# A state-space block followed by an attention-convolution block: scan matmuls on the two halves of the array's rows, and another form of the LayerNorm pass

## The chip, the core and the metric

The kernel runs on one core of a Trainium2 chip. Five engines work side by side, each through its own queue in order: PE (matmuls; PEld is its weight load), DVE (VectorE), ACT (ScalarE), POOL (GpSimd) and SP (SyncE), which here issues nearly all DMAs. The metric is the device time of one execution in microseconds; three runs of the kernel before gave 7110.56 to 7121.52, with a median of 7116.44.

## The reference, cut to what matters

Four images of 96 channels and 128 x 128 pixels pass through two blocks.

```python
# block 1, per image: d = 192 inner channels, L = 128*128
z  = silu(depthwise3x3(in_w @ x))
xs = [z, z^T, flip(z), flip(z^T)]                 # 4 directions k
dts, B, C = split(x_proj[k] @ xs[k], (6, 1, 1))
delta = softplus(dt_w[k] @ dts + dt_b[k])         # 192 channels from 6 rows
h_t = exp(-exp(A_log)*delta_t) * h_(t-1) + delta_t * B_t * xs_t
y   = sum over k of (h * C + D * xs), each turned back
x1  = x + out_w @ layernorm_over_channels(y) + out_b
# block 2, per image: normalise x1, split it by sign (relu_split_norm),
# two 3x3 convolutions make keys and queries, their products make a 3x3
# kernel per image, which convolves a third map; output = several terms summed
```

## The kernel before

**Block 1, projections.** `project` makes z of one image in strips of 8 rows (128 x 512 fp32 matmuls, line 601), stores it (`zb`), and makes the 16 small rows per direction pair that the scans need (`rows_out`, `cols_out`). These are kept as three bf16 pieces whose sum is the fp32 value: `xdt` (6 rows of dt for each direction) and `xbc` (B and C), both in DRAM.

**Block 1, scans.** `ssm_scan` works on pairs of images. The 384 channels of a pair are three groups of 128: group 0 is of the first image alone, group 1 is half of each image, group 2 is of the second image alone. Each group has 4 directions with 16 chunks of 1024 positions: 64 steps a group, 384 steps in all for two pairs, 256 of them of one image alone and 128 of both. Two steps share one load of rows, `xr` (`rows_in`, 4 buffers, issued six steps ahead), and one load of z, `u` (`u_in`). Each step has two halves of 512 positions. Per half there are three matmuls: `pd` = dt (line 750, in `deltas`), and B and C spread over the 128 channels (line 776, in `spread`, PSUM tiles `pBC`, 3 buffers). The contraction holds 60 rows for one image (9 x 6 rows for the three-piece products and 6 for B and C) and 120 for two. So `xr` is loaded by three DMAs of 18 rows and one of 6 rows for each image, each row 2048 positions (4 KB): 4 DMAs for a pair of steps of one image, 8 for a pair of both. After the matmuls: softplus and exp on ACT, three DVE operations per half (lines 803, 820 the scan itself, 824), and two POOL operations per step (799 and 832).

**LayerNorm pass.** `ssm_output` handles one image in 16 chunks of 1024 positions. Of each chunk it forms means of y and y^2 over 192 channels (matmuls with `mean192`, line 927), copies them (937), regroups them by two small DMAs (940, `mq`), makes the reciprocal root (944 to 954), writes it to DRAM (956, `rd`), reads it back broadcast over 96 partitions (964, `r`), and scales the projected chunk (978 to 980). Three chunks are in work at once: the loop body starts chunk c, makes the root of chunk c-1 and projects and scales chunk c-2; y is loaded three chunks ahead. The result goes to `xr` and from there to `xnew` (1015).

**Split norm.** `split_norm` reads `xnew` twice in 16 pieces, the first time for sums (lines 1064 to 1071), the second time to write the two signed maps `x1d`, `x2d` (1139 to 1154). Pieces are loaded three ahead, in 4 buffers, the first ones before the small arithmetic that precedes each pass.

**Order of work.** Generators are interleaved by `co_run(left, right, pace)`: each `yield` of `left` states a cost, and `right` is advanced by that cost times `pace`. A scan step costs 5.2. The scans run beside the projections of images 0, 1 and 2-3 (pace 0.25, 0.75, 1.35), then beside `norm` of image 0, that is `ssm_output` and `split_norm` (pace 0.5), then beside `direct_maps` of image 0 (pace 0.95); what is left is drained. All these instructions keep the order in which they were emitted on each engine (`in_order`). After that come `attend` of images 0 to 3, each with the `norm` of the next image and the output stage of the last one beside it; there the framework's scheduler orders the instructions, with the order of emission as priority.

**Setup.** `scan_weights` fills `wdt` and `wbc` by DMAs that POOL issues (lines 233 and 236); `output_weights` and the first strip of `project` follow.

Of the kernel before, what the change touches and what calls it, by code (L numbers as in the profile page):

```python
# [17 lines left out]
C = 96  # L18
# [42 lines left out]
def kernel(  # L61
# [151 lines left out]
    def scan_weights():  # L213


        wdt = const.tile([KS, 3, NK, 128], BF16, name="wdt", tag="wdt")
        wbc = const.tile([KS, 3, 2, 128], BF16, name="wbc", tag="wbc")
        with tc.tile_pool(name="w0", bufs=1) as w0:
# [8 lines left out]
            for img, ch, g, p, n in PARTS:  # L227
                row = img * KI if g == 1 else 0
                for w in range(3):
                    src = pieces[w].rearrange("p (k c) -> p k c", k=NK)[:, :, ch : ch + n]  # L230
                    for i in range(3):
                        at = row + w * 18 + i * RANK
                        nc.gpsimd.dma_start(wdt[at : at + RANK, g, :, p : p + n], src)
                for q in range(2):
                    at = row + 54 + q
                    nc.gpsimd.dma_start(wbc[at : at + 5 : 2, g, q, p : p + n], one[:, :n])
# [170 lines left out]
    def project(b, weights, stats, beside, zb, xdt, xbc, ps):  # L407
# [9 lines left out]
        with tc.tile_pool(name="a2", bufs=2, side="left") as p2:  # L417
# [81 lines left out]
            def rows_out(z1, z2, s):  # L499
# [26 lines left out]
                def store():  # L526
                    for q in range(2):
                        sl = slice((2 * s + q) * CH, (2 * s + q + 1) * CH)
                        for dst, p, n in ((xdt, 0, 12), (xbc, 12, 4)):
                            at = 32 * q + p  # L530
                            nc.sync.dma_start(
                                dst[0, :, :, sl].rearrange("i r f -> r i f"), rp[at : at + n]
                            )
# [7 lines left out]
            def cols_out(rp, s):  # L541
# [16 lines left out]
                def store():  # L558
                    h = (s - HS + 1) * ZR
                    for dst, r, n in ((xdt, 0, 12), (xbc, 12, 4)):  # L560
                        for i in range(3):
                            to = dst[1, i].rearrange("r (w h) -> w r h", h=H)
# [82 lines left out]
    def ssm_scan(zb, xdt, xbc, yms, ready):  # L645
# [5 lines left out]
        with (  # L651
# [32 lines left out]
            def rows_in(n):  # L684

                if n >= total:
                    return
                g, k = steps[n][:2]
                sl = slice(lows(n) * SN, (lows(n) + 2) * SN)
                imgs = images(g)  # L690
                xr = p1.tile([KS, 2 * SN], BF16, name="xr", bufs=4)
                for a, img in enumerate(imgs):
                    at = a * KI
                    r = k // 2 * RANK
                    src = xdt[img][k % 2, :, r : r + RANK, sl]
                    for w in range(3):
                        nc.sync.dma_start(xr[at + 18 * w : at + 18 * w + 18], src)
                    r = k // 2 * 2
                    src = xbc[img][k % 2, :, r : r + 2, sl]
                    nc.sync.dma_start(xr[at + 54 : at + KI], src)  # L700
                pairs[n] = dict(xr=xr[0 : KI * len(imgs)])
# [35 lines left out]
            def deltas(n):  # L737
                if n >= total:
                    return
                g, k, i, c = steps[n][:4]  # L740
# [4 lines left out]
                xr = pairs[n - n % 2]["xr"]  # L745
                at = (c - lows(n - n % 2)) * SN
                for half in range(2):
                    pd = ps.tile([128, CH], F32, name="pd", bufs=2)
                    sl = slice(at + half * CH, at + half * CH + CH)
                    nc.tensor.matmul(  # L750
                        pd, lhsT=wdt[0 : xr.shape[0], g % 3, k], rhs=xr[:, sl],
                        start=True, stop=True,
                    )
# [17 lines left out]
            def spread(n, q, half):  # L771

                xr = pairs[n - n % 2]["xr"]
                p = ps.tile([128, CH], F32, name="pBC", bufs=3)
                at = (steps[n][3] - lows(n - n % 2)) * SN + half * CH
                nc.tensor.matmul(  # L776
                    p,
                    lhsT=wbc[0 : xr.shape[0], steps[n][0] % 3, q],
                    rhs=xr[:, at : at + CH],
                    start=True,  # L780
                    stop=True,
                )
# [118 lines left out]
    def ssm_output(b, yms, xnew, stats, ps, side):  # L901
# [4 lines left out]

        with tc.tile_pool(name="c2", bufs=2, side=side) as p2:
# [3 lines left out]
            ys, sums_of, near, made = {}, {}, {}, {}  # L911
# [6 lines left out]
            def squares(c):  # L918
                sq = p2.tile([C, 2, SN], F32, name="sq", bufs=1)
                for j in range(2):  # L920
                    nc.scalar.activation(sq[:, j], ys[c][:, j], AF.Square)
                sums_of[c] = sq, bank(ps)

            def sums(c, j):
                sq, pm = sums_of[c]
                for g in range(4):
                    nc.tensor.matmul(
                        pm[32 * g : 32 * g + 32],
                        lhsT=mean192[:, 0:32],
                        rhs=(ys[c], sq)[g % 2][:, j, bass.ts(g // 2, CH)],  # L930
                        start=(j == 0),
                        stop=(j == 1),
                    )

            def rows(c):
                st = p2.tile([128, CH], F32, name="st", bufs=1)
                nc.scalar.copy(st, sums_of.pop(c)[1])
                mq = made[c] = p2.tile([RS, 2, W], F32, name="mq")
                for i in range(2):
                    nc.sync.dma_start(mq[:, i], st[32 * i : 32 * i + 65 : 64])  # L940

            def inverse(c):
                m, q = made[c][:, 0], made[c][:, 1]
                nc.vector.tensor_mul(m, m, m)
                nc.vector.tensor_sub(q, q, m)
                nc.vector.tensor_scalar(q, q, 0.0, None, ALU.max)

            def roots(c):
                q = made[c][:, 1]
                nc.scalar.activation(q, q, AF.Sqrt, bias=eps[0:RS])  # L950

            def back(c):
                q = made.pop(c)[:, 1]
                nc.vector.reciprocal(q, q)
                to = rd[bass.ts(c, SN)]
                nc.sync.dma_start(to.rearrange("(p f) -> p f", f=W), q)
                xr = p2.tile([C, SN], F32, name="xr")
                nc.sync.dma_start(xr, xb[:, bass.ts(c, SN)])
                near[c] = xr, to

            def spread_out(c):
                xr, to = near[c]
                r = p2.tile([C, SN], F32, name="r")
                nc.sync.dma_start(r, to.partition_broadcast(C))
                near[c] = xr, r

            def projected(c, h):
                po = part(ps, C, CH)
                for j in range(2):
                    nc.tensor.matmul(  # L970
                        po, lhsT=outws[:, j], rhs=ys[c][:, j, bass.ts(h, CH)],
                        start=(j == 0), stop=(j == 1),
                    )
                return po

            def scaled(c, h, po):
                xr, r = (t[:, bass.ts(h, CH)] for t in near[c])
                nc.vector.tensor_mul(r, po, r)
                nc.vector.scalar_tensor_tensor(xr, r, outbs, xr, ALU.add, ALU.add)
                nc.vector.bn_stats(stats[:, 2 * c + h], xr)  # L980

            for c in range(3):
                load_y(c)
            yield 2.0
            for c in range(NS + 2):
                new, old = c < NS, c - 2 if c >= 2 else None
                mid = c - 1 if 1 <= c <= NS else None
                if old is not None:
                    po = projected(old, 0)
                yield 1.2  # L990
                if mid is not None:
                    inverse(mid)
                    roots(mid)
                if new:
                    squares(c)
                if old is not None:
                    scaled(old, 0, po)
                    po = projected(old, 1)
                    ys.pop(old)
                if mid is not None:  # L1000
                    back(mid)
                yield 1.4
                if new:
                    sums(c, 0)
                if mid is not None:
                    spread_out(mid)
                yield 1.4
                if old is not None:
                    scaled(old, 1, po)
                    load_y(c + 1)  # L1010
                if new:
                    sums(c, 1)
                yield 1.4
                if old is not None:
                    nc.sync.dma_start(xnew[:, bass.ts(old, SN)], near.pop(old)[0])
                yield 1.4
                if new:
                    rows(c)
                yield 1.4

    def split_norm(xnew, x1d, x2d, stats, keep, cnt, ps, side):


        with tc.tile_pool(name="n2", bufs=2, side=side) as p2:
            ahead = []

            def piece(t):
                if t < NS:
                    y = p2.tile([C, SN], F32, name="xn", bufs=4)
                    nc.sync.dma_start(y, xnew[:, bass.ts(t, SN)])  # L1030
                    ahead.append(y)

            for i in range(3):
                piece(i)
            gs, mv = combine(ps, stats.rearrange("p c s -> p (c s)"), gmean, "gs1")
            a = col("rstd1")
            rsqrt(a, gs[:, 1:2])

            m = col("m1")
            nc.vector.tensor_sub(m, mv[:, 0:1], gs[:, 0:1])  # L1040
# [890 lines left out]
```

## Time and profile before

| | |
|---|---|
| median of three runs | 7116.44 us (7110.56 to 7121.52) |
| profiled execution | 7116.44 us, of which 7114.7 us from the first to the last instruction |
| busy: PE, DVE, ACT, POOL | 5755.4, 4896.6, 3063.5, 3370.6 us |
| mean granted TensorE clock | 0.887 |
| DMA | 1227.33 MB, mean 173 GB/s |

The stages can be told from the lines that run in them: setup to 100 us, projections with scans from 100 to 2216 us, `norm` of image 0 with scans to about 2740 us, `direct_maps` with the remaining scans to about 3735 us, `attend` of image 0 with `norm` of image 1 to about 4180 us, then about 910, 1020 and 890 us for images 1, 2 and 3, and 114 us for the last output stage. A stage's limit is read from the busy time of each engine in that stretch and from what its waits end on; the shares over the whole span are averages over unlike stages.

### The profile page before, as it was taken

The page shows a single profiled execution, that of the slowest core. Times are in us where ns is not written, and L with a number is a line of the kernel's source. Part 1 is how long each engine was busy: PE and PEld are TensorE (multiplying, and loading weights), DVE is VectorE, ACT ScalarE, POOL GpSimd, SP SyncE. Part 2 cuts the span into 40 slices and gives each one's busy share as a digit, 9 for nine tenths or more (in the row PEclk, how much of TensorE's full clock was granted, in tenths as well). Part 3 has the DMA queues.
Part 4 walks back from the last instruction along what each step waited for, and adds up shares of the span by engine and source line. Part 5 has one row for each costly group of instructions (what it writes and reads, how often), then busy time and mean ns, then how long its engine had stood idle before and what let it go on. Part 6 is the DMA issues. An engine that isn't in the chain of part 4 may idle for free. (4 is left out here: it accounts for less than half of the span.)

```text
span 7114.7 us, 73298 instructions
## 1 busy us (share of the span) xinstructions
PE 5755.4 (81%) x22236; PEld 2355.7 (33%) x22236; DVE 4896.6 (69%) x6898; ACT 3063.5 (43%) x3813; POOL 3370.6 (47%) x2050
## 2 busy tenths in 40 slices
PE   4989978888996835889997748997789886788976
PEld 1333322222221112444442224443334443334432
DVE  2247768888886666767756667666876667775587
ACT  1247767677775466556631242223322214222103
POOL 2026657768786224757832234333444343444541
PEclk9999988998997657999997879998989998899998
DMA  4556666665765556565556676665766656665455
GB/s 118 139 147 176 180 193 179 194 197 160 213 176 155 173 174 184 155 182 160 162 169 172 185 210 183 166 174 155 229 176 180 172 163 188 193 186 148 116 152 166
DMA packets 755613, 1227.33 MB, mean 173 GB/s; under 512 B 197986, under 2 KB 507134, under 8 KB 742740
## 3 DMA queue, kind: packets, MB, share of 16 engines
q1 hardware_dynamic: 753028, 1222.37, 61.8%
q8 instruction: 179, 2.93, 0.2%
q14 instruction: 214, 1.75, 0.1%
q0 software_dynamic: 2192, 0.27, 0.1%
HBM read 858.12 MB, written 296.46 MB: 162 GB/s over the span
## 5 line engine op out<-in xcount | busy, mean ns | idle before, releaser
L1247 POOL TENSOR_TENSOR t<-y 128x768 f32<-128x768 f32 (+1 forms) x352 | 562.5, 1598 | 1794.6 <-PE bank L1271 845.2
L799 POOL TENSOR_TENSOR dl<-dl,u 128x1024 f32<-128x1024 f32 x384 | 1006.5, 2621 | 792.7 <-ACT dA L767 471.1
L601 PE MATMUL bank<-y,wp 128*128 128x512 f32 (+3 forms) x3584 | 1328.8, 627 | 65.2 <-DMA y<-y 30.7
L832 POOL TENSOR_TENSOR y<-y,dl 128x1024 f32<-128x1024 f32 x384 | 1053.3, 2743 | 568.2 <-DVE dl L824 530.5
L1271 PE MATMUL bank<-t,wd 128*128 128x384 f32 (+2 forms) x4224 | 1153.9, 499 | 84.7 <-DVE ring L1314 42.7
L820 DVE TENSOR_TENSOR_SCAN dA<-dA,pBC 128x512 f32<-128x512 f32 x768 | 981.6, 1278 | 30.4
L1320 ACT COPY s<-bank 128x384 f32<-128x384 f32 (+2 forms) x292 | 135.3, 463 | 1669.1 <-PE bank L1282 1599.2
L824 DVE TENSOR_TENSOR dl<-dA,pBC 128x512 f32<-128x512 f32 x768 | 528.5, 688 | 414.3 <-PE pBC L776 354.7
L1271 PEld LDWEIGHTS bank<-t,wd 128*128 128x128 f32 (+1 forms) x4224 | 558.8, 170 | 637.1 <-issue 333.3
L776 PE MATMUL pBC<-xr,wbc 60*128 60x512 bf16 (+1 forms) x1536 | 522.4, 405 | 291.7 <-DVE dA L820 247.3
L1629 PE MATMUL bank<-y,wn 128*128 128x384 f32 (+5 forms) x2408 | 671.6, 508 | 58.4 <-DMA y<-x1d 27.5
L601 PEld LDWEIGHTS bank<-y,wp 128*128 128x128 f32 (+3 forms) x3584 | 462.5, 170 | 758.8 <-issue 670.5
L1271 PE MATMUL bank<-t,wa 128*96 128x384 f32 (+1 forms) x1408 | 539.0, 531 | 215.4 <-DVE t L1248 87.4
L643 ACT ACTIVATE dl<-pd,dtb 128x512 f32<-128x512 f32 x768 | 485.3, 684 | 188.9 <-PE pd L750 178.3
L803 DVE TENSOR_TENSOR pBC<-dl,pBC 128x512 f32<-128x512 f32 x768 | 527.0, 686 | 3.6 <-POOL dl L799 2.4
L1312 DVE TENSOR_TENSOR d<-s,bank 128x384 f32<-128x384 f32 (+2 forms) x292 | 155.4, 532 | 435.9 <-ACT s L1320 405.6
L1629 PEld LDWEIGHTS bank<-y,wn 128*128 128x128 f32 (+3 forms) x2408 | 311.9, 169 | 348.4 <-issue 173.9
L767 ACT ACTIVATE dA<-dl,negA 128x1024 f32<-128x1024 f32 x384 | 420.3, 1141 | 2.3
L1271 PEld LDWEIGHTS bank<-t,wa 128*96 128x96 f32 x1408 | 235.5, 180 | 509.9 <-issue 354.0
L643 ACT ACT_TABLE_LOAD x245 | 314.3, 1283 | 183.9 <-PE pd L750 180.8
L1248 POOL TENSOR_TENSOR t<-y 128x384 f32<-128x384 f32 (+1 forms) x352 | 372.2, 1057 | 0.0
L1249 POOL TENSOR_TENSOR t<-y 128x384 f32<-128x384 f32 (+1 forms) x352 | 368.3, 1046 | 0.0
(247 smaller groups left out, 7645.8 us busy)
## 6 DMA issues: line engine op xcount, KB each, us to landing
u<-zb SPq DMA_DIRECT2D x192, 1024.0 KB
xr<-xdt SPq DMA_DIRECT2D x768, 72.0 KB
yms<-y SPq DMA_DIRECT2D x96, 512.0 KB
y<-yms SPq DMA_DIRECT2D x64, 768.0 KB
xn<-xnew SPq DMA_DIRECT2D x128, 384.0 KB
y<-y SPq DMA_DIRECT2D x128, 258.2 KB
zb<-z SPq DMA_DIRECT2D x64, 512.0 KB
y<-vd SPq DMA_DIRECT2D x168, 193.8 KB
```

The costliest lines, as they stand in the source:

```text
L601: nc.tensor.matmul(blocks(pz[p:e]), lhsT=ws[k][:, d, c : c + e - p], rhs=window(ys[k], at, d, n), start=(i == 0), stop=(i == len(terms) - 1),)
L643: nc.scalar.activation(dst, src, AF.Softplus, bias=bias)
L767: nc.scalar.activation(live[m]["dA"], live[m]["dl"], AF.Exp, scale=negA[:, g % 3, k : k + 1])
L776: nc.tensor.matmul(p, lhsT=wbc[0 : xr.shape[0], steps[n][0] % 3, q], rhs=xr[:, at : at + CH], start=True, stop=True,)
L799: nc.gpsimd.tensor_mul(t, t, u_view(n))
L803: nc.vector.tensor_mul(p, live[n]["dl"][:, bass.ts(half, CH)], p)
L820: nc.vector.tensor_tensor_scan(h, h, p, init, ALU.mult, ALU.add)
L824: nc.vector.tensor_mul(live[n]["dl"][:, sl], live[n]["dA"][:, sl], live[n]["C", half])
L832: nc.gpsimd.tensor_add(v, v, t.rearrange("p (a b) -> p a b", b=W))
L1247: eng.tensor_sub(v[:, 0:2], of(y, 0), of(y, 2))
L1271: nc.tensor.matmul(pc[p:e, :n], lhsT=w[:, i, c : c + e - p], rhs=t[k][:, i, :n], start=(k == 0), stop=False,)
L1629: nc.tensor.matmul(pc[p:e, :n].rearrange("p (h w) -> p h w", w=W), lhsT=w[:, c : c + e - p], rhs=v[:, :, 0:W], start=(i == 0), stop=(i == ...
```

## The change

Five things change.

1. **Groups of one image.** The weights `wdt` and `wbc` are held twice, in rows 0 to 59 and rows 64 to 123. The first half of each chunk is loaded to rows 0 to 59 of `xr` and the second half to rows 64 to 123, so that the matmuls of the two halves use the two halves of the array's rows. `deltas` and `spread` emit such matmuls in pairs, as before. Groups of both images keep their 120 rows.
2. **Loads of `xr`.** `xdt` is laid out so that 18 rows lie one after the other; one DMA with a broadcast writes 54 rows. For one image a pair of steps needs 4 pieces with 2 DMAs each (rows of 512 positions, 1 KB); for both images 2 pieces with 2 DMAs each (4 KB rows). The stores to `xdt` become two of 6 rows in place of one of 12.
3. **LayerNorm pass.** One chunk's sums and roots and the projection of the chunk before it make up the loop body; the steps are put off by ticks of a `Later` queue. y is loaded two chunks ahead, at the end of a loop body, and the result is written over y. `r` and x share one tile.
4. **Split norm.** Pieces are loaded one ahead, in 2 buffers, the first one after the small arithmetic.
5. **Pace.** The scans beside `norm` of image 0 get 0.25 in place of 0.5.

```diff
-        wdt = const.tile([KS, 3, NK, 128], BF16, name="wdt", tag="wdt")
-        wbc = const.tile([KS, 3, 2, 128], BF16, name="wbc", tag="wbc")
+        wdt = const.tile([128, 3, NK, 128], BF16, name="wdt", tag="wdt")
+        wbc = const.tile([128, 3, 2, 128], BF16, name="wbc", tag="wbc")
...
-            for img, ch, g, p, n in PARTS:
-                row = img * KI if g == 1 else 0
+            for row, ch, g, p, n in (
+                (row, *part)
+                for img, *part in PARTS
+                for row in ((KI * img,) if part[1] == 1 else (0, 64))
+            ):
...
-                        for dst, p, n in ((xdt, 0, 12), (xbc, 12, 4)):
+                        for dst, p, n in (
+                            (xdt[0, 0], 0, 6), (xdt[0, 1], 6, 6), (xbc[0], 12, 4)
+                        ):
...
-                for a, img in enumerate(imgs):
-                    at = a * KI
-                    r = k // 2 * RANK
-                    src = xdt[img][k % 2, :, r : r + RANK, sl]
-                    for w in range(3):
-                        nc.sync.dma_start(xr[at + 18 * w : at + 18 * w + 18], src)
+                if alone:
+
+                    pieces = [
+                        (imgs[0], 64 * h, low + i * SN + h * CH, CH, i * CH)
+                        for h in range(2) for i in range(2)
+                    ]
+                else:
+                    pieces = [(img, KI * a, low, 2 * SN, 0) for a, img in enumerate(imgs)]
+                for img, row, a, m, at in pieces:
+                    src = xdt[img][k % 2, k // 2].rearrange("i r f -> (i r) f")[:, a : a + m]
+                    nc.sync.dma_start(
+                        xr[row : row + 54, at : at + m],
+                        src.unsqueeze(0).to_broadcast([3, 3 * RANK, m]),
+                    )
                     r = k // 2 * 2
-                    src = xbc[img][k % 2, :, r : r + 2, sl]
-                    nc.sync.dma_start(xr[at + 54 : at + KI], src)
+                    src = xbc[img][k % 2, :, r : r + 2, a : a + m]
+                    nc.sync.dma_start(xr[row + 54 : row + KI, at : at + m], src)
...
+            def to_psum(n, half, p, w):
+
+                pair = pairs[n - n % 2]
+                xr = pair["xr"]
+                step = steps[n][3] - lows(n - n % 2)
+                if pair["alone"]:
+                    rows, at = slice(64 * half, 64 * half + KI), step * CH
+                else:
+                    rows, at = slice(0, KS), step * SN + half * CH
+                nc.tensor.matmul(
+                    p, lhsT=w[rows], rhs=xr[rows, at : at + CH], start=True, stop=True
+                )
...
+                def sums():
+                    for j in range(2):
+                        for g in range(4):
+                            nc.tensor.matmul(
+                                pm[32 * g : 32 * g + 32],
+                                lhsT=mean192[:, 0:32],
+                                rhs=(y, sq)[g % 2][:, j, bass.ts(g // 2, CH)],
+                                start=(j == 0),
+                                stop=(j == 1),
+                            )
+                    later(lambda: nc.scalar.copy(st, pm))
+                    later(rows, 1)
+
+                def rows():
+                    for i in range(2):
+                        nc.sync.dma_start(mq[:, i], st[32 * i : 32 * i + 65 : 64])
+                    later(inverse, 1)
+
+                def inverse():
+                    nc.vector.tensor_mul(m, m, m)
+                    nc.vector.tensor_sub(q, q, m)
+                    nc.vector.tensor_scalar(q, q, 0.0, None, ALU.max)
+                    nc.scalar.activation(q, q, AF.Sqrt, bias=eps[0:RS])
+                    nc.vector.reciprocal(q, q)
+                    later(back)
+
+                def back():
+                    to = rd[bass.ts(c, SN)]
+                    nc.sync.dma_start(to.rearrange("(p f) -> p f", f=W), q)
+                    near[c] = p2.tile([C, 2, SN], F32, name="rx")
+                    nc.sync.dma_start(near[c][:, 1], xb[:, bass.ts(c, SN)])
+                    later(lambda: nc.sync.dma_start(near[c][:, 0], to.partition_broadcast(C)))
+
+                nc.scalar.activation(sq, y, AF.Square)
+                later(sums, 1)
...
+            for c in range(NS + 1):
+                if c < NS:
+                    deviations(c)
+                later.tick()
                 yield 1.4
+                later.tick()
                 yield 1.4
...
+                for h in range(2):
...
+                        later(scaled, 1)
+                        if h:
+                            to = xnew[:, bass.ts(c - 1, SN)]
+                            later(lambda t=t, to=to: nc.sync.dma_start(to, t), 2)
+                    later.tick()
+                    yield 1.4
+                later.tick()
                 yield 1.4
+                later.tick()
+                load_y(c + 2)
                 yield 1.4
...
+            ahead = piece(0)
             for i in range(NS):
-                y = ahead.pop(0)
-                piece(i + 3)
+                y = ahead
+                if i + 1 < NS:
+                    ahead = piece(i + 1)
...
-    co_run(left, last, 0.5)
+    co_run(left, last, 0.25)
```

## The prediction

> **What bounds the kernel now.** I first cut the span into its stages and read the busy time of each engine in each (the table of windows: start and end, length, then PE, PEld, DVE, ACT and POOL busy with counts, granted clock, DMA share, GB/s).
>
> ```profile
> 525.00:960.00 435.00, 398.98 (x1431) 132.00 (x1430) 309.74 (x397) 298.05 (x344) 263.03 (x97) 0.96 0.67 178
> 960.00:1540.00 580.00, 468.30 (x1520) 160.08 (x1518) 462.25 (x566) 388.26 (x448) 406.33 (x158) 0.89 0.69 196
> 1540.00:2216.00 676.00, 602.39 (x1973) 186.42 (x1974) 594.54 (x718) 508.20 (x587) 557.35 (x208) 0.91 0.63 178
> 2216.00:2740.00 524.00, 265.21 (x604) 61.43 (x600) 341.18 (x467) 291.08 (x338) 143.56 (x92) 0.57 0.60 176
> 2740.00:3180.00 440.00, 372.92 (x1477) 184.79 (x1478) 293.77 (x357) 231.62 (x298) 293.05 (x111) 0.91 0.58 166
> 3180.00:3640.00 460.00, 442.52 (x1807) 200.70 (x1805) 357.75 (x438) 282.22 (x364) 336.35 (x127) 0.98 0.59 171
> 4060.00:4180.00 120.00, 35.46 (x102) 14.78 (x102) 82.45 (x143) 82.98 (x99) 17.89 (x43) 0.60 0.78 229
> ```
>
> The scan steps in a stage are half its matmuls of line 750 (same windows, that line alone): 47, 78, 104, 29, 53 and 60 in the first six rows. The first row is image-alone steps and PE is busy 92%. The second is steps of both images: no engine is over 81%. The third is alone again: PE 89%, DVE 88%, and 6.5 us a step where POOL's two operations take 557.35 / 104 = 5.4 us. The fourth is `norm` of image 0: nothing is near full, so a chain of waits sets it. In the fifth (both) and sixth (alone) PE is at 85% and 96%.
>
> The timeline of a scan step says what an alone pair costs on PE:
>
> ```profile
> 1765.16 0.11 PEld L776 LDWEIGHTS <-wbc 60*128 60x128 bf16 x2 [0.76 <-issue]
> 1765.17 0.60 PE L776 MATMUL pBC<-xr,wbc 60*128 60x512 bf16 x2
> 1765.70 0.30 PEld L601 LDWEIGHTS bank<-y,wp 128*128 128x128 f32 x2 [0.42 <-issue]
> ```
>
> Two matmuls of 0.38 us take 0.60: the second adds about 0.22. The longer gap ahead of a 60-row load (0.76, against 0.24 ahead of a 120-row one at 1164 us) is there already.
>
> In `norm` of image 0 I followed one chunk:
>
> ```profile
> 2420.36 0.28 SPq L956 DMA_DIRECT2D rd<-mq  x1
> 2420.74 0.33 SPq L958 DMA_DIRECT2D xr<-in_x  x1
> 2421.60 0.72 SPq L964 DMA_DIRECT2D r<-rd  x1
> 2422.41 0.38 SPq L916 DMA_DIRECT2D y<-yms  x1
> ...
> 2423.37 0.38 SPq L1015 DMA_DIRECT2D xnew<-xr  x1
> ```
>
> ```profile
> 2432.55 0.28 DVE L944 TENSOR_TENSOR mq<-mq 8x128 f32<-8x128 f32 x1 [7.46 <-DMA mq<-st]
> ```
>
> The `mq` DMAs are issued right after, from 2423.85, and land 8 us later though they hold 8 KB: they queue behind the y, r and xnew transfers. Root, squares (which stand behind the root on ACT), sums, copy and `mq` form a loop of 16 us a chunk (line 944 starts at 2416.54 and 2432.55). So even three chunks at once are held by this loop.
>
> Last, POOL's setup:
>
> ```profile
> 62.98 2.98 POOL L236 DMA_DIRECT2D wbc<-one  x6
> 65.94 8.23 POOL L233 DMA_DIRECT2D wdt<-piece  x15
> 74.40 11.31 POOL L233 DMA_DIRECT2D wdt<-piece  x21 [0.23 <-issue]
> 90.83 2.28 POOL L423 MEMSET y<- 96x1292 f32 x2 [4.03 <-PE pb L254]
> ```
>
> PE's output weights (89.97 us) and the first strip (loaded at 92.02 us) wait for the end of this row.
>
> **What the Trainium skill says.** TensorEngine Tiling (Array Packing), Key Properties: tiles on different rows load and multiply in parallel, and a change of tiling mode drains the array. No run shows row halves yet; the trace has column halves at work (twelve 128*64 fp32 matmuls in 2.79 us at 1705 us, against three 128*128 ones in 1.45 us at 1700 us) and the drain (0.76 against 0.24). TensorE: Matmul & The Clock Gate, Measured speedup vs the span model: a pack lasts one matmul and about 4 ns for each further one, so I estimate 0.38 us in place of 0.60 for a pair. DMA: Bandwidth & Descriptors, Queues, rings and completion order: each engine consumes descriptors in ring order; the 8 us of `mq` agree. The same page, Anatomy of one DMA: waits happen on the issuing sequencer, so a waiting SP holds every later transfer; SP's list of waits has 130.0 us in 2290 to 2572 us on line 956 for the reciprocal.
>
> **The change, part by part.** The profiled execution is the median run: 7116.44 us, its span 7114.7.
>
> *Setup.* `wdt` goes from 4 x 9 = 36 to 54 DMAs, `wbc` from 8 to 12: 18 x 0.547 (line 233) + 4 x 0.508 (line 236) = 11.9 us, all ahead of the first strip. **+12**; I see no cover, bounds +10 to +14.
>
> *Pairs on PE.* 256 alone steps have 3 pairs each, each saving up to 0.22 us. Where the second waits for its PSUM buffer (line 776 waits for DVE 221 times in 1536) it saves little: I take 80%. First row: 47 x 3 x 0.22 x 0.8 = 25 us. Third: 104 x 3 x 0.22 x 0.8 = 55 us. Sixth: 60 steps give 32 us. Lower bound nothing, if the halves don't overlap. In the third row DVE (88%) and POOL are close behind, so I count 20 of 55; in the others PE binds, so nearly all.
>
> *SP.* An `xr` DMA costs SP 0.67 us and about 0.05 to the next. An alone pair of steps goes from 4 to 8 (+2.9 us), a pair of both from 8 to 4 (-2.9, more where issues were held up: three took 4.3 us at 1157 us). Summed from the timeline, SP's issues fill about 260 of 435, 450 of 580 and 400 of 676 us in the first three rows, and some 85% and 75% of the fifth and sixth. After: alone rows go to about 75%, 83% and, in the sixth, (345 + 30 x 2.9) / 460 = 94%. In the second row POOL waits 104 us for `u`, DVE 47 for image pieces, ACT 40 for strips, all queued on SP: this is what SP at that load does, and its relief gains, I take 25 of these 190. The price in alone rows: 10 us each in the first and third, 30 in the sixth. The `xdt` stores add 128 x 0.32 = 41 us of SP over the projections, in its slack.
> Projections: -15 (first) - 25 (second) - 10 (third) = **-50**, bounds -130 and +50.
>
> *`norm` of image 0.* The new loop has a second cycle, through SP. The store of chunk c-1 waits for the scaling; then SP waits for this store to land, since y of chunk c+2 takes its buffer; then come y, rd of chunk c, x, and the broadcast, which the scaling of c needs. At the stage's 176 GB/s a 384 KB tile takes 2.2 us and y (768 KB) 4.5, plus 1.7 us to landing (line 233). So: issue 0.4, store 3.9, y issue 0.4, rd behind y 4.9, issues 0.7, x and broadcast 6.1, scaling 2 x (0.67 + 0.75 + 0.69) = 4.2: 20.6 us against 16 now. 17 x 20.6 = 350 against 282 (2290 to 2572): +68. Nearest bounds: if the landings hide, the 16 us loop stays (272, -10); at 25 us a chunk +143. The pace takes half of the stage's 24 co-run scan steps away (244 of cost x 0.25 / 5.2 = 12): some 12 x 5.3 = 64 us of DVE and as much of ACT, mostly in idle time; I count -25. `split_norm` has ACT at work in 145 of 168 us; fewer scans offset the shallower loads, but each refill is exposed: +7. **+50**, bounds -40 and +130.
>
> *`direct_maps`.* It takes the 12 steps. Alone, line 1629 runs 253 matmuls in 95 us. At that rate the fifth row's 980 take 368 of 440 us, so a step costs 1.4 us or more there; by the busiest 100 us (333 at 3600) it is 2.7. 12 x 2 = +24. Both-image steps gain SP time (-15), alone steps -30 by PE and +30 by SP: **+10**, bounds -50 and +90.
>
> *`norm` of image 1.* It lies beside a short attend, PE is at 71% and then 30% (last row). The scheduler may order SP better: I take half of the LayerNorm loss, 30, and 10 for loads one ahead. A piece now waits for the buffer of the one before last: about 6 us landing + 2.7 of ACT for two, near today's 4 us each. **+40**, bounds 0 and +100.
>
> *`norm` of images 2 and 3.* PE is 88 to 90% busy over 4180 to 4880 and 5090 to 5880 us, beside the LayerNorm, and hides it; in the tails (4880 to 5090, 5880 to 6110 us) PE is at 69% and loads show: **+20**, bounds 0 and +80.
>
> Sum: 12 - 50 + 50 + 10 + 40 + 20 = +82, so **7198 us**.
>
> **Rivals.** (a) *Pairs and fewer issues win.* For it: PE at 89 to 96% in alone rows and 190 us of SP-fed waits in the second; against: DVE and POOL at 6 us a step. Projections -120, norm 0 and 1 at -20 and +10, maps -40, rest +5: 12 - 120 - 20 + 10 - 40 + 5 = -153: 6963 us. It decides if a paired matmul takes under 0.1 us more than one and the second row loses over half its waits. (b) *The LayerNorm loop is no longer than now*, as it is today bound by `mq`: norm 0 at 0, image 1 +10, rest +10: 12 - 50 + 0 + 10 + 10 + 10 = -8: 7108 us. (c) *SP fills up in alone steps*: projections +45, maps +50: 12 + 45 + 50 + 50 + 40 + 20 = +217: 7333 us. For it, the 94%; against, `xr` is issued six steps ahead. (d) That the halves don't overlap costs 20 + 25 + 30 us more: inside (c)'s range.
>
> **How the numbers follow.** Forecast 0.47, (a) 0.17, (b) 0.18, (c) and (d) 0.18. The forecast's own range is 7140 to 7260. The range 7010 to 7340 leaves out 0.12 of (a) and 0.07 of (c). A measurement tells about 0.2%, 14 us, from no change. Faster: 0.16 of (a) and 0.07 of (b) = 0.23; within: 0.06 of (b) and 0.02 of the forecast = 0.08; slower: the rest, 0.69.
>
> **What would show it.** First strip at 104 us. Line 776 pairs of 60 rows at 0.38 to 0.40 us together. At most 13 us for a pair of steps in the third row's place, as now. Line 944 (its successor) every 20 us in `norm` of image 0, with SP waiting on `xnew` landings ahead of y. If that interval is 16 us, the largest term is wrong; if `u` waits grow past 100 us in alone steps, the SP term is.

## The result and the profile after

The changed kernel takes 7381.15 us (median of four runs, 7373.39 to 7392.91), the kernel before 7118.98 beside it: a ratio of 1.0357, 95% interval 1.0312 to 1.0402. It is slower by 262 us where I forecast 82. The profiled execution took 7392.91 us, span 7391.1.

The table of windows of the kernel after, cut at the same work as the first six rows shown of before and at the attend of image 0 (columns: stretch, length, busy PE, PEld, DVE, ACT, POOL with counts, clock, DMA share, GB/s):

```profile
540.00:986.00 446.00, 381.93 (x1422) 126.13 (x1420) 308.23 (x395) 294.07 (x338) 260.25 (x96) 0.92 0.63 172
986.00:1614.00 628.00, 480.47 (x1526) 161.25 (x1527) 463.90 (x568) 391.82 (x452) 405.89 (x159) 0.86 0.67 181
1614.00:2327.00 713.00, 580.23 (x1969) 177.61 (x1969) 587.00 (x718) 508.04 (x587) 553.08 (x208) 0.88 0.60 170
2327.00:2870.00 543.00, 216.99 (x532) 51.89 (x528) 278.00 (x396) 225.77 (x253) 90.94 (x70) 0.58 0.52 149
2870.00:3440.00 570.00, 464.73 (x1825) 225.73 (x1825) 365.27 (x446) 301.86 (x381) 347.07 (x133) 0.89 0.59 157
3440.00:3910.00 470.00, 415.19 (x1785) 192.40 (x1786) 351.10 (x430) 277.07 (x360) 331.00 (x125) 0.94 0.57 165
4300.00:4420.00 120.00, 35.75 (x94) 14.52 (x94) 72.21 (x134) 77.89 (x91) 10.48 (x37) 0.60 0.70 204
```

No engine got more work: PE in the third row went from 602.39 to 580.23 us; the pairs overlap there, as the last part shows. But the row takes 713 us in place of 676, and both-image steps (second row) 628 in place of 580 with nearly the same busy times. All engines wait more.

POOL waits longer for `u`. Its waits for it in the third row's stretch, before and after (us in total, times, longest):

```profile
POOL dl L799 <- DMA u<-zb: 16.4, 6, 4.0
```

```profile
POOL dl L815 <- DMA u<-zb: 77.8, 25, 10.2
```

In the sixth row they went from 46.5 to 80.9 us. `u` is loaded by SP. Here is SP in the alone steps of the kernel after, by its timeline (start, duration):

```profile
1859.10 0.85 SPq L741 DMA_DIRECT2D u<-zb  x1
1860.05 0.73 SPq L711 DMA_DIRECT2D xr<-xdt  x1
1860.83 0.71 SPq L717 DMA_DIRECT2D xr<-xbc  x1
...
1864.46 0.68 SPq L711 DMA_DIRECT2D xr<-xdt  x1
1865.73 0.67 SPq L717 DMA_DIRECT2D xr<-xbc  x1
1866.50 0.72 SPq L536 DMA_DIRECT2D xdt<-rp  x2
```

Eight row loads take 6.4 us, and whatever follows stands behind them. Summed from this view, SP's issues fill 75% and 77% of the first and third rows, against 60% and 58% before, and 87% of the sixth, against 74%.

The stages of all kernels below, from their traces, in us. "Steps" counts by the starts of POOL's first operation of a scan step (line 799 of before): 0 to 63 and 128 to 239 are alone steps, 64 to 127 both-image steps; they lie within the projections but for the last few us, and the projections also hold the time before the first step. "Norm 0" runs from the last matmul of the projections to the first of `direct_maps`, "maps" to its last, "norm 1" from there to the first `wd` matmul, with which the attend of image 1 starts, and "rest" to the end. Each row is of one trace: steps 128 to 239 took 736 to 742 us in before, norm_alone and norm_free_y, whose scans are the same, so a difference of some 5 us there means little.

| kernel | steps 0-63 | 64-127 | 128-239 | projections | norm 0 | maps | norm 1 | rest | median us |
|---|---|---|---|---|---|---|---|---|---|
| before | 682 | 476 | 740 | 2116 | 531 | 961 | 482 | 2923 | 7119 |
| after | 700 | 508 | 788 | 2213 | 549 | 1044 | 520 | 2951 | 7381 |
| scans_alone | 698 | 511 | 788 | 2211 | 544 | 991 | 489 | 2915 | 7257 |
| norm_alone | 684 | 482 | 736 | 2119 | 600 | 949 | 510 | 2945 | 7216 |
| pace_half | 701 | 509 | 782 | 2209 | 600 | 997 | 507 | 2956 | 7370 |
| merged_loads | 685 | 506 | 747 | 2157 | 543 | 967 | 489 | 2930 | 7195 |
| split_stores | 683 | 493 | 747 | 2140 | 534 | 956 | 488 | 2918 | 7144 |
| cut_loads | 702 | 508 | 781 | 2208 | 549 | 999 | 487 | 2932 | 7265 |
| nine_engines | 678 | 428 | 741 | 2063 | 516 | 888 | 493 | 2935 | 6989 |
| merged_nine | 681 | 423 | 739 | 2060 | 519 | 896 | 492 | 2931 | 7002 |
| pairs_nine | 700 | 423 | 778 | 2120 | 528 | 930 | 498 | 2912 | 7100 |
| cut_nine | 700 | 428 | 786 | 2132 | 529 | 932 | 495 | 2912 | 7095 |
| more_issues | 689 | 425 | 776 | 2109 | 524 | 930 | 487 | 2911 | 7063 |
| pairs_whole | 667 | 419 | 749 | 2053 | 525 | 896 | 496 | 2914 | 7005 |
| norm_free_y | 684 | 479 | 742 | 2122 | 587 | 950 | 506 | 2945 | 7206 |
| rows_in_order | 687 | 414 | 736 | 2054 | 518 | 883 | 484 | 2927 | 6960 |

### The profile page after: what moved, and what is told of

Read it like the earlier page. It is cut to its first block, busy times and chain, and to the rows that moved or that the text cites. A ratio compares the mean times of both kernels' runs of the same rounds, so it can differ in the third digit from the quotient of the medians.

```text
span 7391.1 us, 73827 instructions
## 1 busy us (share of the span) xinstructions
PE 5708.6 (77%) x22236; PEld 2341.9 (32%) x22236; DVE 4881.0 (66%) x6898; ACT 3058.9 (41%) x3739; POOL 3350.8 (45%) x2072
## 5 line engine op out<-in xcount | busy, mean ns | idle before, releaser
L608 PE MATMUL bank<-y,wp 128*128 128x512 f32 (+3 forms) x3584 | 1350.2, 636 | 82.8 <-DMA y<-y 37.2
L1628 PE MATMUL bank<-y,wn 128*128 128x384 f32 (+5 forms) x2408 | 695.7, 525 | 73.5 <-DMA y<-x1d 38.8
L729 PE MATMUL pBC<-xr,wbc 60*128 60x512 bf16 (+1 forms) x1536 | 440.6, 406 | 325.3 <-DVE dA L836 274.3
```

The costliest lines, as they stand in the source:

```text
L608: nc.tensor.matmul(blocks(pz[p:e]), lhsT=ws[k][:, d, c : c + e - p], rhs=window(ys[k], at, d, n), start=(i == 0), stop=(i == len(terms) - 1),)
L729: nc.tensor.matmul(p, lhsT=w[rows], rhs=xr[rows, at : at + CH], start=True, stop=True)
L1628: nc.tensor.matmul(pc[p:e, :n].rearrange("p (h w) -> p h w", w=W), lhsT=w[:, c : c + e - p], rhs=v[:, :, 0:W], start=(i == 0), stop=(i == ...
```

## The experiments

The kernel before ran beside each set of runs: 7119 to 7127 us, and 7116 beside the last.

**Which half of the change, and the pace.** *scans_alone* has points 1 and 2 of the change, *norm_alone* points 3 and 4, *pace_half* all but point 5:

```diff
-    co_run(left, last, 0.25)
+    co_run(left, last, 0.5)
```

> The scan half of the change alone: row halves, row loads, stores and setup of the changed kernel, with LayerNorm, its loads and the pace as before. Theory 1 (the extra issues on SP in alone steps slow the scans): the projections end about 110 us later than before, as in the changed kernel, and direct_maps takes 20 to 40 us longer than 961: 7240 to 7290 us. Rival (the scans are slowed by the order of the LayerNorm part or by displaced steps): within 30 us of the 7119 before.

> The LayerNorm half alone, one chunk at a time and loads one ahead, with the scans and the pace of 0.5 as before. Theory 1: projections as before (first matmul of norm at about 2216 us), the LayerNorm loop 300 to 330 us against 282, norm of image 1 +40 and of images 2 and 3 +35: 7190 to 7240 us. Rival (the loop hides wherever the scans are not slowed as well): 7120 to 7150 us.

> The changed kernel with the pace of norm of image 0 set back from 0.25 to 0.5. Theory A (direct_maps is set by its scan steps, so each step that the pace moves there costs its full 6 to 7 us): norm of image 0 gets up to 30 us longer, direct_maps 70 to 80 us shorter, the whole 40 to 60 us shorter, 7320 to 7340. Theory B (direct_maps is set by loads on SP and not by the number of steps): norm longer by 30, maps shorter by 20 or less, 7380 to 7400.

scans_alone took 7257.29 us, ratio 1.0187 (1.0150 to 1.0224), norm_alone 7216.41, 1.0129 (1.0095 to 1.0163). So the halves cost 137 and 96 us, nearly additive. Nearly all that projections and a third of what `direct_maps` lost belongs to the scan half. pace_half took 7370.43, 1.0339 (1.0306 to 1.0373), within the interval of the changed kernel, and met neither theory: `norm` of image 0 is 50 us longer and `direct_maps` 47 shorter. The pace only moves time from one stage to the other.

**Merging and splitting without row halves.** *merged_loads* is before with one 54-row load an image, *split_stores* before with only the stores split, as the new layout needs:

```diff
-for w in range(3):
-    nc.sync.dma_start(xr[at + 18 * w : at + 18 * w + 18], src)
+nc.sync.dma_start(xr[at : at + 54], src.unsqueeze(0).to_broadcast([3, 18, 2 * SN]))
```

```diff
-for dst, p, n in ((xdt, 0, 12), (xbc, 12, 4)):
+for dst, r, p, n in ((xdt, 0, 0, 6), (xdt, 6, 6, 6), (xbc, 0, 12, 4)):
```

> The kernel before with only its row loads merged: for each image one 54-row broadcast in place of three 18-row loads, and the stores split in two for it; no row halves, so 2 loads a pair in alone steps and 4 in both-image steps, in place of 4 and 8. Theory 1 (the number of issues on SP is the price): the both-image steps 64 to 127, 477 us before and 508 after, fall to 450 to 470, the alone rows gain 5 to 15 us each, the whole 7040 to 7100. Theory 2 (the merged broadcasts or the split stores hold up what is queued behind them): steps 64 to 127 take 500 us or more, the whole 7150 to 7200.

> The kernel before with only the stores of the dt rows split in two of 6 rows each, as the changed kernel has them (128 more stores in the projections); loads, layout and all else as before. Theory S (the stores cost): steps 64 to 127 take 500 us or more, as with the merged loads, against 477, and the whole is 40 to 75 us slower, 7160 to 7195. Theory L (the merged loads cost, by the three DMA engines that they run on): steps 64 to 127 within 8 us of 477, the whole within 20 us of 7119.

merged_loads took 7195.19 us, 1.0096 (1.0060 to 1.0131): half the row loads in every step, and slower. Both-image steps went from 476 to 506 us, as in the changed kernel. split_stores took 7143.76, 1.0022 (1.0010 to 1.0033). The stores are some 17 us of these 75; the merged loads are the rest. split_stores met neither theory in full: the stores alone brought both-image steps from 476 to 493 us, over half of what merged_loads lost there, though each takes SP only some 0.3 us. SP's waits in both-image steps, before and in merged_loads:

```profile
SPq L459 <- DMA xr<-xdt: 22.0, 29, 1.6
```

```profile
SPq L533 <- DMA xr<-xdt: 34.6, 13, 3.7
SPq L459 <- DMA xr<-xdt: 30.3, 11, 4.9
```

The time SP gained by issuing less it lost at once in the next DMA, a strip's copies (459) or the row store (533), until the row loads had landed. That speaks against the issues as the limit there, and for the transfers; the next runs decide.

**How many DMA engines carry a row load.** The packet records show a row load of before as 4096-byte packets of mostly 159 ns. Such packets in flight, every 0.3 us over the four loads of one alone pair (60 packets, kernel before):

```
us      1793.5 .8 1794.1 .4 .7 1795.0 .3 .6 .9 1796.2 .5 .8 1797.1 .4
packets      3  3      3  3  3      3  3  3  3      3  3  3      3  1
```

It is three for 88% of this time and never over four. The Trainium skill states this (DMA: Bandwidth & Descriptors, Rules for kernel authors): an outermost dimension of fewer than 16, for instance a leading broadcast of c copies, confines the whole DMA to at most c engines. The source of before is 3 pieces x 6 rows, that of the changed kernel 3 copies x 18 rows: three engines in both. A pair of both-image steps puts 2 x 18 packets, 5.7 us, on each of the three, in 476 / 32 = 14.9 us, that is 38%. All 16 engines are at 67% on average in these steps, 7 of it from these loads (5.7 x 3 / 16 / 14.9), so I estimate the three at 60 + 38 = 98%. This takes it that every load uses the same three and that all else is spread evenly; the records do not name the engine.

*nine_engines* has the new layout, whose 18 source rows are one dimension, and loads it three times as before; *merged_nine* loads it once, with the copies innermost and the weights' rows to match:

```diff
-    src = xdt[img][k % 2, :, r : r + RANK, sl]
+    src = xdt[img][k % 2, k // 2].rearrange("i r f -> (i r) f")[:, sl]
```

```diff
-    nc.sync.dma_start(xr[at : at + 54], src.unsqueeze(0).to_broadcast([3, 18, 2 * SN]))
+    nc.sync.dma_start(xr[at : at + 54], src.unsqueeze(1).to_broadcast([18, 3, 2 * SN]))
```

> Layout and split stores of the changed kernel, but three loads of 18 rows an image as before; since the 18 source rows are now one dimension, I expect the packets of one load to run nine abreast and not three. Theory L: the three engines that carried the row loads are relieved, steps 64 to 127 at 477 us or less, the whole 7040 to 7110. Theory S: the split stores still cost, steps 64 to 127 about 500, the whole 7160 to 7195.

> One load an image again, as in the merged loads kernel, but with the rows in another order (the three copies of a row side by side, the weights to match), so that its slowest dimension is 18 and its packets run nine abreast. Theory L: steps 64 to 127 at 450 to 475 us, the whole 7020 to 7090, under both kernels. If the number of issues and the stores decide and not the engines, it is as the merged loads kernel, 7195.

nine_engines took 6988.63 us, 0.9805 (0.9785 to 0.9826), merged_nine 7001.84, 0.9816 (0.9795 to 0.9836), both faster than expected. Both-image steps fell to 428 and 423 us, `direct_maps` to 888 and 896; alone steps hardly moved. POOL's waits for `u` in steps 64 to 127, before and in nine_engines, fell to a third. Of the time with any such packet in flight, three were in flight for 65% before; now it is 11%, and 7 to 9 for 34%:

```profile
POOL dl L799 <- DMA u<-zb: 92.0, 24, 9.7
```

```profile
POOL dl L802 <- DMA u<-zb: 28.9, 9, 7.8
```

nine_engines alone leaves a rival: its loads are also issued faster, in a median of 0.32 us in place of 0.67. merged_nine rules it out. It differs from merged_loads only in the order of the copies (and of the weights' rows), reads the same rows from the same places, and its row loads take no less to issue (median 0.80 against 0.70 us), yet it is 193 us faster.

**What the eight DMAs of an alone pair cost.** *cut_loads* is merged_loads, *cut_nine* merged_nine, with each alone load cut in four by columns; *pairs_nine* is scans_alone over nine engines:

```diff
+m = 2 * SN // (1 if len(imgs) == 2 else 4)
+for o in range(0, 2 * SN, m):
     # the two loads, for columns o to o + m
```

> The merged loads kernel (7195 us) with each load of an alone pair cut in four by columns: 8 DMAs of 1 KB rows a pair, as in the changed kernel, but all into one set of rows, with no row halves and no second set of weights. If the pairs of matmuls gain what I forecast (0.22 us for each), the alone steps here are slower than in the scan half of the change by about 20 us over the 64 first and 40 over steps 128 to 231, and the whole is at 7270 to 7320. If the pairs gain nothing and the 8 DMAs are the price, the alone steps run as there (64 first in about 697 us, steps 128 to 231 in about 738) and the whole is at 7230 to 7250. If the row halves themselves are the price, the alone steps stay as in the merged loads kernel (685 and 697 us), 7190 to 7205.

> The merged nine kernel (7002 us) with each load of an alone pair cut in four by columns, 8 DMAs a pair, no row halves. If the number of issues has a price of its own (6 more of 0.7 us a pair on SP), 7040 to 7080; if it cost only by the three engines, 7000 to 7020. Against the row halves with nine engines: if the pairs of matmuls gain what I forecast, those are 20 to 60 us faster than this; if nothing, they are about 12 slower, which is their setup.

> The scan half of the change (7257 us) with its row loads over nine engines, the rows in the order of the merged nine kernel; LayerNorm and pace as before. If the three engines are what made the scans slow, it falls by about as much as the merged loads did (193 us), to 7050 to 7100, below the 7119 before. If the 8 DMAs of an alone pair are the price whatever engines they use, only the both-image steps gain: 7150 to 7200.

cut_loads took 7265.49 us, 1.0185 (1.0164 to 1.0206): between two of the ranges as a whole, but within 8 us of scans_alone in every stage up to "norm 1", though it has no row halves. cut_nine took 7094.54, 0.9960 (0.9946 to 0.9974), and pairs_nine 7100.20, 0.9966 (0.9951 to 0.9982): again the same, within 13 us in every stage. cut_nine lost more than I had expected. So the alone steps are as slow as their eight DMAs make them, with or without the pairs of matmuls. pairs_nine is at the edge of its first range, but its stages are those of the second theory: both-image steps fell from 511 to 423 us, alone steps stayed (698 and 788 us, now 700 and 778). This price stays, 93 us from merged_nine to cut_nine, whatever engines carry the loads.

**Issues or small packets; and pairs with room on SP.** *more_issues* adds six tiny loads an alone pair to merged_nine, *pairs_whole* feeds each row half with a whole pair of steps (four DMAs of 4 KB rows in place of eight of 1 KB):

```diff
+for o in range(6):
+    nc.sync.dma_start(more[:, o], xbc[img][k % 2, :, r : r + 2, lo + 16 * o : lo + 16 * o + 16])
```

```diff
-(imgs[0], 64 * h, low + i * SN + h * CH, CH, i * CH) for h in range(2) for i in range(2)
+(imgs[0], 64 * h, low, 2 * SN, 0) for h in range(2)
```

> The merged nine kernel (7002 us) with six more loads for each alone pair, of 6 rows of 16 columns (192 bytes in all) into a tile that nothing reads. The work is not changed; the six stand for the six more issues of the cut loads without their bytes. If SP's issues are the price, it loses as much as cutting did, 70 to 95 us: 7070 to 7100. If the small packets are, it stays at 7000 to 7020.

> The row halves with nine engines (7100 us), but each half of the rows loaded with the whole pair of steps: 4 DMAs of 4 KB rows an alone pair in place of 8 of 1 KB, at twice the bytes. By the price of cutting (93 us for six more issues a pair), 2 more issues than the merged nine kernel cost about 31, and the setup 12: 7045 if the pairs of matmuls gain nothing. If they gain 25 to 60 once SP has room, 6985 to 7020.

more_issues took 7062.84 us, 0.9938 (0.9918 to 0.9959), a little less than the 7070 to 7100 that stood for the issues: 61 of the 93 us (1.2 of 1.4% against the kernel before beside each), and 37 of 47 in steps 128 to 239, come without the bytes. POOL's waits for `u` in those steps, in merged_nine, more_issues and cut_nine:

```profile
POOL dl L804 <- DMA u<-zb: 5.8, 5, 2.1
```

```profile
POOL dl L810 <- DMA u<-zb: 63.7, 15, 7.1
```

```profile
POOL dl L807 <- DMA u<-zb: 96.2, 22, 11.8
```

pairs_whole took 7004.59, 0.9828 (0.9803 to 0.9854), as merged_nine, and so in the range that stood for a gain of the pairs. Steps 128 to 239 in merged_nine and pairs_whole, by the table of windows:

```profile
1428.00:2160.00 732.00, 654.13 (x2151) 203.28 (x2152) 644.30 (x779) 552.19 (x640) 597.12 (x226) 0.91 0.64 182
```

```profile
1424.00:2168.00 744.00, 622.68 (x2154) 191.00 (x2151) 645.84 (x782) 553.91 (x640) 597.78 (x227) 0.89 0.71 198
```

PE has 31 us less to do and the stretch is not shorter: DVE, with 645 us of work, is now ahead of PE, and PE's waits for DVE's scan to free its PSUM tiles went from 38.1 to 60.0 us. But POOL's waits for `u` also grew, from 5.8 to 30.0, and what the two more issues a pair do was not told apart from this. Only in steps 0 to 63 do the pairs gain, 681 to 667 us. With their setup and two more issues it comes to nothing as a whole; that the pairs gain as much as my price for the issues (31 us) and the setup would need is not shown, since that price may be too high for two.

**The LayerNorm loop.** *norm_free_y* is norm_alone with the scaled chunk written elsewhere than over y:

```diff
-    t = y[:, 0]
+    t = rx[:, 0]
```

> The LayerNorm half alone (7216 us) with the scaled output written over the broadcast tile in place of over y, so that y of chunk c+2 need not wait until the store of chunk c-1 has landed. If SP's cycle through that store sets the loop, as forecast, the interval of a chunk in norm of image 0 falls from 19.9 us to 16 to 17.5, and the whole to 7140 to 7180. If the way from the root over rd to the broadcast and the scaling sets it, the interval stays within 1 us, 7200 to 7225.

It took 7206.38 us, 1.0106 (1.0083 to 1.0128), not to be told from norm_alone; a chunk takes 19.0 us in place of 19.9. SP no longer waits for the store ahead of y, and then waits for the reciprocal instead. One turn of the loop in the kernel after, by its timeline:

```profile
2519.27 0.94 DVE L965 RECIPROCAL mq<-mq 8x128 f32<-8x128 f32 x1 [0.47 <-ACT mq L964]
2520.48 0.32 SPq L932 DMA_DIRECT2D y<-yms  x1
2520.90 0.30 SPq L970 DMA_DIRECT2D rd<-mq  x1
...
2526.38 0.30 SPq L973 DMA_DIRECT2D rx<-rd  x1
...
2531.49 0.69 DVE L1003 TENSOR_TENSOR y<-bank,rx 96x512 f32<-96x512 f32 x1 [5.50 <-DMA rx<-rd]
...
2535.09 0.31 SPq L1012 DMA_DIRECT2D xnew<-y  x1
...
2535.70 0.26 DVE L961 TENSOR_TENSOR mq<-mq 8x128 f32<-8x128 f32 x1
```

rd lands 5.5 us after its issue, the broadcast 5.1 us after its own, the scaling of both halves takes 4.2, and DVE holds the next chunk's root until the scaling is done. With the root and the issues ahead of rd, 2.9 us more, that is the loop: 17.7 us in this turn.

**A version faster than both.** *rows_in_order* is before with rows stored as (row, copy) in place of (copy, row): the store stays whole, a load's 18 rows are one dimension, and the B and C rows too.

```diff
-dram.tile([2, 3, n, L], BF16)
+dram.tile([2, n, 3, L], BF16)
-src = xdt[img][k % 2, :, r : r + RANK, sl]
+src = xdt[img][k % 2, r : r + RANK, :, sl].rearrange("r i f -> (r i) f")
```

> A version to beat both: the kernel before with the rows stored as (row, copy) in place of (copy, row), so that one store of 12 rows suffices as before and the 18 source rows of a load are one dimension; the B and C rows, 6 in one dimension, should run six abreast. Three loads an image and no row halves. Theory L: the nine engines kernel less its split stores, 6960 to 6990. If the stores and the B and C rows matter nothing, 6989.

It took 6960.39 us, 0.9764 (0.9744 to 0.9783): 163 us under the 7123 of before beside it, at the low end of what was expected. Of the 28 us under nine_engines, what the whole stores give and what the B and C rows give was not told apart.

## Why the prediction was wrong

The working asked for +82 and the span grew by 276. Point by point, profiled spans:

- *Setup*: forecast +12, measured +14. The last clearing of the first strip on POOL starts at 104.49 us against 90.83:

```profile
104.49 2.28 POOL L426 MEMSET y<- 96x1292 f32 x2 [3.93 <-PE pb L257]
```

- *Projections*: forecast -50, measured +97. **This is the step that failed**, in all of its parts. "In the second row ... its relief gains, I take 25": both-image steps lost 32 us. The relief was worth nothing, because what held SP there was the three DMA engines, not the count of issues: over three engines the merged loads gained nothing (merged_loads, 506 us), over nine they brought these steps to 423 (merged_nine). The `xdt` stores, put "in its slack", cost 17 us there (split_stores). "The price in alone rows: 10 us each in the first and third": the alone steps 0 to 63 and 128 to 239 lost 18 and 48 us, and the same eight DMAs without row halves (cut_loads) lost 20 and 41. SP's share was forecast well (83% in the third row, measured 77%), its price was not: at that share `u` comes late.
- *What the pairs are worth*, within the same sum: 25 us in the first row and 20 in the third were too much for this kernel. scans_alone against cut_loads is 4 us faster in steps 0 to 63 and 7 slower in 128 to 239. With room on SP (pairs_whole against merged_nine) it is 14 faster and 10 slower.
- *Pairs on PE*: the mechanism was right, though PE's busy time in the third row fell by 22 us where 55 was written. In the alone steps of the kernel after, two 60-row matmuls take as long as one, as the Trainium skill has it (TensorEngine Tiling (Array Packing), Key Properties):

```profile
1872.78 0.39 PE L729 MATMUL pBC<-xr,wbc 60*128 60x512 bf16 x2
1873.01 0.38 PE L729 MATMUL pd<-xr,wdt 60*128 60x512 bf16 x2
```

- *norm of image 0*: forecast +50, measured +18. The size of the loop was near: 68 + 7 = 75 forecast, and +69 measured at the old pace (norm_alone), with 19.9 us a chunk against 20.6. That was luck in part. The cycle I drew began with the store of xnew; norm_free_y takes this store out of the way of y, and a chunk still takes 19.0. The parts from rd to the scaling were sized well (15.9 us forecast, 14.8 in the turn above); the root and DVE's order take the place of the store. The mis-sized term is the pace: it took 50 us from the stage, not 25.
- *direct_maps*: forecast +10, measured +83. The moved steps cost 47 us where "12 x 2 = +24" was written; most of the rest is the scan half's +30, the same error as in the projections. The 2 us a step came in part from a misread window. The prediction's "line 1629 runs 253 matmuls in 95 us" counts 3640 to 3735 us, but `direct_maps` ends at 3709:

```profile
3640.00:3735.00 95.00, 60.04 (x253) 32.09 (x252) 0.96 0.50 132
3640.00:3709.00 69.00, 59.27 (x251) 31.86 (x251) 1.00 0.50 129
```

At 251 in 69 us the fifth row's 980 take 269 of 440 us, a step costs (440 - 269) / 53 = 3.2 us, and 12 of them 39.
- *norm of image 1*: forecast +40, measured +37. *Images 2 and 3*: +20, measured +28.

The sum of the measured terms, 14 + 97 + 18 + 83 + 37 + 28, is 277. Rival (c), SP filling up in alone steps, was the nearest, at 7333, and still named only half of it. My sign for it was not set well: `u` waits reached 77.8 and 80.9 us in the third and sixth rows, each under the 100 that I had asked for, together well over it, and I had not said which counts.

What stays open: why one load of 54 rows costs 58 us more than three of 18 when three engines carry them (merged_loads against split_stores), and 13 when nine do, which is within the scatter of the runs. The longer waits of the next DMA on SP were seen; that they are the cause was only argued. Up to a third of the price of cutting an alone load does not come from the issues and was not taken apart. The granted clock was lower in the changed kernel, 0.88 against 0.91 in the third row; whether that adds to the loss or follows from PE's waiting was not tested, but more_issues lost its 37 us in steps 128 to 239 at 0.90 against 0.91 in merged_nine.

## What to carry to other kernels

A queue that looks busy may be held by what it feeds: before counting issues, look at how many packets of a DMA are in flight. A pattern whose slowest dimension is small, as 3 here, can fill a few DMA engines while the average says 67%; reordering dimensions so that a larger one comes first was worth more here than anything the change did on PE. And an operation made cheaper on an engine at 90% gains only where no other engine has as much to do in that stretch, while each added DMA delays what stands behind it in its queue: in more_issues 768 loads of 0.67 us, 515 us of SP's time, cost 61 us of the kernel's.

## What the runs showed of the hardware

- The time of an issue on SP doesn't follow the bytes: 0.67 us was the median for 18 rows and for 6 rows of 4 KB in before, and the mean for the 192-byte loads of more_issues, against 0.37 (median) for the load of y (768 KB).
- It does follow how the source is laid out: the same 18 rows as one dimension were issued in a median of 0.32 us in place of 0.67 (nine_engines, both-image steps), and 6 rows in 0.30 (rows_in_order). Nine engines alone do not bring it: the loads of merged_nine took 0.80.
- Two matmuls on 60 rows each, on the two halves of the array's rows, took 0.38 to 0.39 us together (kernel after), against 0.60 on the same rows (kernel before).
